# A two-layer graph network on one Trainium2 core: one-hot matrices of targets kept in 8 bits between the layers, and four more edge groups sorted

## The chip, the cores and the metric

The kernel runs on one core of one Trainium2 chip. The metric is the device time of one execution in microseconds (us). The median of three timed runs of the kernel before is 2827.05 us (2824.18 to 2834.32).

## The reference

There are 6250 nodes of 64 features and 206250 edges, sorted by their target. Two message-passing layers follow each other, each behind a layer norm and a relu and each with a residual:

```
h = relu(layernorm(x))
msg = relu(h[src] + edge_attr_16 @ W_edge.T + b_edge)
agg = segment_sum(msg, dst)
u = (h + agg) @ W1.T + b1;  u = relu(batchnorm(u)) @ W2.T + b2;  x = x + u
h = relu(layernorm(x))
msg = relu(concat(h[src], edge_attr_64) @ M_W.T + M_b)
z = segment_sum(msg, dst)
x = x + relu(concat(h, z) @ U_W.T + U_b)
```

The second layer needs, per edge, the same source and the same target as the first.

## The kernel before, in words

Edges come in NG = 101 groups of 16 tiles of 128 edges, 1612 tiles in all. The first GS = 73 groups are **sorted**: each tile's rows are scattered into a table `place` in HBM, into SB = 36 blocks by target (128 targets to a block), and in a block into 50 tiles by source. The other 28 groups are **direct**: their source rows are fetched by an indirect DMA for each tile.

*Layer 0, stage A (the loop at L929).* For each sorted group, `places` and `rank` (VectorE) compute where rows go, `rows` copies the attributes into a tile `to` of 4 buffers (ScalarE L824, L829), and `scatter` issues 16 indirect DMAs from GpSimd (L840). After each part of a group, `Blocks.step` pushes one item of a finished block, at most four in a group. An item is up to 8 tiles of 128 edges: 50 tiles make 6 items of 8 tiles and one of 2. `Line.push` runs its stages two pushes deep. `prepare` makes `hot_s`, the one-hot matrix of sources, in bf16 (L434). `gather` multiplies it into the node table split into three bf16 parts, which is 24 matmuls to a full item. `targets` makes `hot_d`, the one-hot matrix of targets, in f32 (VectorE L459). `messages` adds and applies the relu. `keep` casts `hot_s` to 8-bit floats (ScalarE L440) and stores it in `hots` in HBM. `sums`, in a later push, multiplies messages and `hot_d` into the block's sums.

*Layer 0, stage B (`unsorted`, L1046).* For each direct group GpSimd issues 16 gathers (L545), and two halves of 8 tiles go through the `Direct` class, each with a `hot_d` of its own (L595). Up to two sorted items stand ahead of each half, as long as there are any.

*Layer 1 (`unsorted` again).* A sorted item loads its 8-bit `hot_s` as `st` (6 buffers, L348 to L351), uses it as it is for the 24 matmuls, makes `hot_d` again on VectorE (L459) from the target column of the block's rows `eb` (loaded whole for each block, 2 buffers), adds its message on VectorE (L470) and applies the relu on ScalarE (L471). Four items stand ahead of each direct half, six in the first two slots, in which no direct half is due. `hot_d` and `msg` have 3 buffers here. A gather waits for a point in TensorE's work one slot back (`pace`).

TensorE, VectorE and ScalarE run in the order in which the program is written (`manual_schedule`), and so do the loads and stores that SyncE issues (`load`, L139): an instruction that waits holds all that is behind it. Blocks of `place` are filled with -1 (`fill`) before rows are scattered into them.

Of the kernel before, what the change touches and what calls it, by code (L numbers as in the profile page):

```python
# [40 lines left out]
F8 = mybir.dt.float8e4  # L41
# [5 lines left out]
P = 128  # L47
# [14 lines left out]
T = NB + 1  # L62
RW = D + ED + 2
SRC = D + ED
DST = SRC + 1
SB = 36
GS = 73
ND = NG - GS
REGION = P * T
ROWS = SB * REGION  # L70
K = 2 * NB
# [8 lines left out]
def window(g):  # L80

    return min(max((g * GT * P * N // E - 31) // P, 0), SB - 2)


LAST = [max(g for g in range(GS) if window(g) <= d <= window(g) + 1) for d in range(SB)]
FIRST = [min(g for g in range(GS) if window(g) <= d <= window(g) + 1) for d in range(SB)]


def begin(g):

    return min((g * GT + GT // 2) * P * N // E - P // 2, NP - P)


DB = begin(GS) // P
LATEST = [max(g for g in range(GS, NG) if begin(g) < (d + 1) * P) for d in range(DB, NB)]


@with_exitstack
def gnn_kernel(
# [24 lines left out]
    nc = tc.nc  # L124

    const = ctx.enter_context(tc.tile_pool(name="const", bufs=1))
    dram = ctx.enter_context(tc.tile_pool(name="dram", bufs=1, space=bass.MemoryType.DRAM))
# [4 lines left out]
    zero = until_1.enter_context(tc.tile_pool(name="zero", bufs=2))  # L132
    pools = [zero, None]
# [5 lines left out]
    def load(to, what):  # L139

        i = nc.sync.dma_start(to, what)
        return tc.keep_in_program_order(i) if in_order[0] else i
# [9 lines left out]
    def turn_slot():  # L152
        slots.append(list(products))
        products.clear()
# [8 lines left out]
    def bank(shape, name, tag, bufs=1, dtype=F32):  # L163
        return ps.tile(shape, dtype, name=name, tag=tag, bufs=bufs)
# [144 lines left out]
    def turned(attrs, n):  # L309

        p = bank([P, P], "at_p", "tr")
        at = zero.tile([P, P], F32, name="at", bufs=3)
        nc.tensor.transpose(p[:n * ED, :], attrs.rearrange("p t f -> p (t f)"), ident)
        nc.scalar.copy(at[:n * ED, :], p[:n * ED, :])  # L314
        return at
# [4 lines left out]


    src_rows = dram.tile([SB, T * P], BF16, name="src_rows")
    hots = dram.tile([P, SB, T * P], F8, name="hots")

    def columns(layer, d, eb):

        if layer == 0:
            p = bank([T, P], "st_p", "tr")
            nc.tensor.transpose(p, eb[:, :, SRC], ident)
            cols = zero.tile([T, P], BF16, name="cols")  # L330
            nc.scalar.activation(cols, p, AF.Identity, bias=shift[:, d:d + 1])
            load(src_rows[d, :].rearrange("(t p) -> t p", p=P), cols)
        dl = work.tile([P, T, 1], F32, name="dl")
        nc.vector.tensor_scalar(dl[:, :, 0], eb[:, :, DST], float(-P * d), None, op0=OP.add)
        attrs = None
        if layer == 0:
            attrs = zero.tile([P, T, ED], F32, name="attrs")
            nc.scalar.copy(attrs, eb[:, :, D:D + ED])
        return dl, attrs

    def sources(layer, d, c):


        a, b = CH[c]
        if layer == 0:
            st = zero.tile([P, 8, P], BF16, name="st", bufs=6)
        else:
            st = pools[1].tile([P, 8, P], F8, name="st", bufs=6)  # L348
        to = st[:, :b - a, :].rearrange("p t q -> p (t q)")
        if layer == 1:  # L350
            load(to, hots[:, d, a * P:b * P])  # L351
        else:
            row = src_rows[d, a * P:b * P]
            load(to, bass.AP(tensor=row.tensor, offset=row.offset, ap=[[0, P], [1, (b - a) * P]]))
        return st
# [26 lines left out]
    class Line:  # L382
# [10 lines left out]
        def push(self, item):  # L393
            now, self.now = (item, None) if self.straight else (self.now, item)
            if self.straight and item:
                item.prepare()
            if now:
                now.gather()
                now.targets()
            if self.later:  # L400
                self.later.pop(0)()
            if self.now:
                self.now.prepare()
            if now:
                now.messages()
            if self.now:
                self.now.keep()
            self.gathered.append(now)
            if len(self.gathered) > self.lag:
                last = self.gathered.pop(0)  # L410
                if last:
                    last.sums()
                    self.later = last.after[:1] + self.later + last.after[1:]
# [5 lines left out]
    class Sorted:  # L419
# [7 lines left out]

        def prepare(self):
            a, n, st = self.a, self.n, self.st
            self.hot_s = st  # L430
            if self.layer == 0:
                self.at = turned(self.attrs[:, a:self.b, :], n)
                self.hot_s = hot_s = zero.tile([P, 8, P], BF16, name="hot_s", bufs=2)
                nc.vector.tensor_scalar(hot_s[:, :n, :], st[:, :n, :], pcol, None, op0=OP.is_equal)  # L434

        def keep(self):

            n = self.n
            hot_8 = zero.tile([P, 8, P], F8, name="hot_8")
            nc.scalar.copy(hot_8[:, :n, :], self.hot_s[:, :n, :], saturate=False)  # L440
            load(hots[:, self.d, self.a * P:self.b * P],
                 hot_8[:, :n, :].rearrange("p t q -> p (t q)"))

        def gather(self):
# [11 lines left out]
        def targets(self):  # L456
            n = self.n
            self.hot_d = pools[self.layer].tile([P, 8, P], F32, name="hot_d", bufs=2 + self.layer)
            nc.vector.tensor_tensor(self.hot_d[:, :n, :],  # L459
                                    slot_p[:, None, :].to_broadcast([P, n, P]),  # L460
                                    self.dl[:, self.a:self.b, :].to_broadcast([P, n, P]),
                                    op=OP.is_equal)
# [78 lines left out]
    def gather(table, g, pool, bufs, lag):  # L541
        gat = pool.tile([P, GT, D], F32, name="gat", bufs=bufs)
        for t in range(min(GT, FULL - g * GT)):
            k = (g - GS) * GT + t
            i = nc.gpsimd.indirect_dma_start(  # L545
# [22 lines left out]
    class Direct:  # L568
# [9 lines left out]
        def prepare(self):  # L578
            pass

        def keep(self):
            pass

        def gather(self):
# [100 lines left out]
    acc = const.tile([P, NP], F32, name="acc")  # L685
# [7 lines left out]
    with tc.tile_pool(name="sort", bufs=1) as sort:  # L693
# [219 lines left out]
        for j0, j1 in chunks:  # L913
            n = j1 - j0
# [12 lines left out]
        steps = Blocks(0, line, loaded, lambda d: slot[0] - LAST[d] - 1, finish_0)  # L927
        with tc.manual_schedule(engines=ordered):
            for g in range(1, GS):  # L929
# [7 lines left out]
                d = window(g) + 3  # L937
                if d < SB and d not in fills:
                    fill(d)
                if g + 2 < GS:  # L940
# [4 lines left out]
                    to = rows(g + 2)  # L945
# [26 lines left out]
    p = bank([P, P], "most_p", "tr")  # L972
# [69 lines left out]
    p = bank([P, P], "b2_p", "tr")  # L1042
# [3 lines left out]
    def unsorted(layer, table, steps, per_half, behind, window_of, done):  # L1046

        with ExitStack() as stack:  # L1050
            pool = stack.enter_context(tc.tile_pool(name=f"unsorted{layer}", bufs=1))
            pools[1] = pool
            stack.enter_context(tc.manual_schedule(engines=ordered))
            line = steps.line
            gats, eas = {}, {}
            left = list(range(DB, NB))
            for g in range(GS, NG + behind):
                turn_slot()
                if g == GS and layer == 1:
                    slots.clear()  # L1060
                if g < NG:
                    gats[g] = gather(table, g, pool, 4 + layer, 1)
                if g > GS and g <= NG:
                    eas[g - 1] = attributes(layer, g - 1, pool)
                c = g - behind
                pd = Bank("pd", ("rk", "pa")[g % 2]) if layer else Bank("pd", "rk")
                for h in range(2):
                    for _ in range(per_half + 2 * layer * (c < GS)):
                        steps.step()
                    if c < GS:  # L1070
                        continue
                    now = []
                    if h == 1:
                        now = [d for d in left if LATEST[d - DB] <= c
                               and (d >= SB or steps.i == len(steps.list))]
                        left = [d for d in left if d not in now]
                    after = [f for d in now for f in done(d)]
                    line.push(Direct(layer, c, h, gats[c], eas[c], pd, window_of(c), pool, after))
            while steps.step():
                pass  # L1080
            line.later += [f for d in left for f in done(d)]
            line.flush()
# [49 lines left out]
    table1 = dram.tile([NP, D], F32, name="table1")  # L1132
# [147 lines left out]
    line_1 = Line(2, True)  # L1280
    line_1.later += [f for n in nodes for f in n.plain()]
    steps = Blocks(1, line_1, lambda d: load_block(d)[0], lambda d: 3, finish_1)
    unsorted(1, table1[:, :], steps, 4, 2, lambda g: acc[:, begin(g):begin(g) + P], update)

    def more_1(k, b, delta, pool):
        node = ds(b * P + k * NH * P, P)
# [75 lines left out]
```

## Time and profile before

The profiled execution took 2824.5 us, with a span of 2822.7 us.

| stretch of the span | what runs | us |
|---|---|---|
| 31.8 to 1602.6 | 1168 scatters on GpSimd (stage A) | 1570.8 |
| 1608.8 to 2163.2 | 444 gathers of layer 0 (stage B) | 554.4 |
| 2163.2 to 2225 | batch norm, layer norm, node table of layer 1 | 62 |
| 2225 to 2787.1 | 444 gathers of layer 1 | 562 |
| 2787.1 to 2822.7 | last items, outputs, end | 35.6 |

| 100 us from | PE | DVE | ACT | POOL | granted clock | DMA share |
|---|---|---|---|---|---|---|
| 900 (of 300, a third) | 71.0 | 62.8 | 35.0 | 76.9 | 0.86 | 0.79 |
| 1900 | 59.4 | 21.2 | 12.4 | 75.5 | 0.77 | 0.32 |
| 2400 | 94.4 | 99.6 | 35.8 | 75.8 | 1.00 | 0.78 |

A busy time is the time in which the engine executes. GpSimd's 75 to 77 of 100 is all that it reaches, because 0.30 us of issue stand between two of its indirect DMAs. The DMA share is the mean busy share of the core's 16 DMA engines.

### The profile page before, as it was taken

Reading aid. Unit: us, or ns where it says so; the run is one execution under the profiler, and the core shown is the slowest. Engines: PE = TensorE matmul, PEld = TensorE weight load, DVE = VectorE, ACT = ScalarE, POOL = GpSimd, SP = SyncE. Lnnn points to the kernel's source line nnn. Section 1 sums busy time; section 2 is a strip of 40 time slices with the busy share of each in tenths; the row PEclk is TensorE's granted clock in tenths of the full one; section 3 lists DMA queues with packets and bytes.
Section 4 is the critical chain, followed back from the end, with each engine's and each line's share of the span. In section 5 each row is a group of like instructions: output and inputs, shape, how many; then the busy total and the mean of one; then the engine's idle time right before and its main releaser. Section 6 shows DMA issues by size and latency. Waiting matters only on the chain. (4 is left out here: it accounts for less than half of the span.)

```text
span 2822.7 us, 57117 instructions
## 1 busy us (share of the span) xinstructions
PE 1974.5 (70%) x20820; PEld 1540.6 (55%) x20820; DVE 1693.4 (60%) x3624; ACT 848.2 (30%) x1637; POOL 2051.0 (73%) x2066
## 2 busy tenths in 40 slices
PE   2366667567766766756677498656565699999887
PEld 2354555455554655545556366444343577878776
DVE  7755656565755756665666244222222599999887
ACT  2232333233333333323334233111111223333332
POOL 5777777777777777777777677777775377777773
PEclk8687888788988988878889799677777899999999
DMA  9877886878888878677776664333332487787764
GB/s 221 199 217 192 233 223 177 207 210 228 210 215 220 225 216 225 192 201 213 222 220 200 179 199 125 90 82 88 87 84 72 144 272 261 247 269 254 249 229 130
DMA packets 343316, 545.17 MB, mean 193 GB/s; under 512 B 114416, under 2 KB 248944, under 8 KB 333808
## 3 DMA queue, kind: packets, MB, share of 16 engines
q1 hardware_dynamic: 270256, 461.35, 55.8%
q0 software_dynamic: 65792, 78.27, 11.4%
q10 hardware_dynamic: 6976, 1.80, 0.4%
q8 instruction: 166, 2.72, 0.4%
q14 instruction: 126, 1.03, 0.1%
HBM read 362.45 MB, written 178.74 MB: 192 GB/s over the span
## 5 line engine op out<-in xcount | busy, mean ns | idle before, releaser
L840 POOL DMA_INDIRECT place<-to,ix x1168 | 1197.4, 1025 | 398.1 <-issue 262.0
L545 POOL DMA_INDIRECT gat<-table,src_d x888 | 845.6, 952 | 331.6 <-issue 181.6
L459 DVE TENSOR_TENSOR hot_d<-cbank,dl 128x1024 f32<-128x1024 f32 (+1 forms) x504 | 556.2, 1104 | 540.6 <-PE pa L148 415.6
L148 PE MATMUL pa<-hot_d,msg 128*64 128x128 f32 (+1 forms) x5400 | 719.3, 323 | 16.6 <-ACT msg L471 15.3
L148 PEld LDWEIGHTS pa<-hot_d,msg 128*64 128x64 f32 (+1 forms) x5400 | 556.4, 163 | 80.6 <-ACT msg L471 25.3
L148 PE MATMUL gp<-we,at 128*128 128x512 f32 (+1 forms) x504 | 293.1, 667 | 401.3 <-ACT at L314 401.3
L148 PEld LDWEIGHTS gp<-we,at 128*128 128x128 f32 (+1 forms) x504 | 90.5, 215 | 420.0 <-ACT at L314 412.9
L148 PEld LDWEIGHTS <-hot_s 128*128 128x128 bf16 x5400 | 222.5, 106 | 160.8 <-issue 143.1
L440 ACT CAST hot<-hot_s 128x1024 fp8e4<-128x1024 bf16 (+1 forms) x252 | 240.6, 955 | 128.7 <-DMA hots<-hot 73.3
L471 ACT ACTIVATE msg<-msg 128x512 f32<-128x512 f32 (+1 forms) x252 | 147.0, 584 | 305.0 <-DVE msg L470 292.3
L608 DVE TENSOR_TENSOR msg<-pm_d,gat 128x512 f32<-128x512 f32 (+1 forms) x56 | 38.4, 686 | 327.8 <-DMA gat<-table,src_d 326.8
L148 PE MATMUL gp<-tab,hot_s 128*128 128x64 bf16 x5400 | 231.8, 205 | 0.0
L148 PE MATMUL gp<-tab,st 128*128 128x64 bf16 x5400 | 205.1, 195 | 32.7 <-DVE msg L470 12.4
L148 PEld LDWEIGHTS <-st 128*128 128x128 fp8e4 x5400 | 176.3, 99 | 77.4 <-issue 63.8
L148 PE MATMUL pm_d<-we,ea_d 128*128 128x512 f32 x112 | 93.1, 926 | 167.2 <-DVE msg L608 167.2
L824 ACT COPY to<-raw 128x288 f32<-128x288 f32 x73 | 31.7, 434 | 589.5 <-DMA place<-to,ix 541.4
L148 PEld LDWEIGHTS pm<-we,ea 128*128 128x128 f32 x1168 | 164.6, 207 | 18.4 <-ACT to L824 11.7
L148 PE MATMUL pm<-we,ea 128*128 128x128 f32 x1168 | 166.5, 291 | 11.6 <-DMA ea<-in_ea 11.6
L470 DVE TENSOR_TENSOR msg<-gp,eb 128x512 f32<-128x512 f32 (+1 forms) x252 | 158.0, 627 | 4.1 <-PE gp L148 3.9
L595 DVE TENSOR_TENSOR hot_d<-cbank,rel_d 128x1024 f32<-128x1024 f32 x112 | 135.4, 1209 | 20.5 <-PE pa L148 13.0
L468 ACT ACTIVATE msg<-gp 128x512 f32<-128x512 f32 (+1 forms) x252 | 140.1, 556 | 11.3 <-PE gp L148 9.9
L609 ACT ACTIVATE msg<-msg 128x512 f32<-128x512 f32 (+1 forms) x56 | 35.1, 626 | 348.0 <-DVE msg L608 347.4
(181 smaller groups left out, 2247.4 us busy)
## 6 DMA issues: line engine op xcount, KB each, us to landing
eb<-place SPq DMA_DIRECT2D x72, 2050.0 KB
place<-minus SPq DMA_DIRECT2D x180, 410.0 KB
st<-src_rows SPq DMA_DIRECT2D x216, 256.0 KB
ea<-in_ea SPq DMA_DIRECT2D x73, 512.0 KB
hots<-hot SPq DMA_DIRECT2D x216, 128.0 KB
st<-hots SPq DMA_DIRECT2D x216, 128.0 KB
place<-to,ix POOLq DMA_INDIRECT x1168
ea_d<-in_ea SPq DMA_DIRECT2D x28, 512.0 KB
```

Of the source, the lines that this page charges most:

```text
L148: i = nc.tensor.matmul(*args, **kwargs)
L440: nc.scalar.copy(hot_8[:, :n, :], self.hot_s[:, :n, :], saturate=False)
L459: nc.vector.tensor_tensor(self.hot_d[:, :n, :], slot_p[:, None, :].to_broadcast([P, n, P]), self.dl[:, self.a:self.b, :].to_broadcast([P, ...
L468: nc.scalar.activation(msg[:, :n, :], gp[:, :n, :], AF.Relu)
L470: nc.vector.tensor_add(msg[:, :n, :], gp[:, :n, :], self.eb[:, self.a:self.b, 0:D])
L471: nc.scalar.activation(msg[:, :n, :], msg[:, :n, :], AF.Relu)
L545: i = nc.gpsimd.indirect_dma_start(out=gat[:, t, :], out_offset=None, in_=table, in_offset=bass.IndirectOffsetOnAxis(ap=src_d[:, k:k + 1], ...
L595: nc.vector.tensor_tensor(self.hot[:, :n, :], slot_p[:, None, :].to_broadcast([P, n, P]), rel_d[:, self.k:self.k + n, None].to_broadcast([ ...
L608: nc.vector.tensor_add(msg, self.pm[:, :n, :], self.gat[:, half, :])
L609: nc.scalar.activation(msg, msg, AF.Relu)
L824: nc.scalar.copy(to[:, :, D:RW], raw)
L840: i = nc.gpsimd.indirect_dma_start(out=place[:, :], out_offset=bass.IndirectOffsetOnAxis(ap=ix[:, t:t + 1], axis=0), in_=to[:, t, :], in_o ...
```

## The change

Layer 0 stores both one-hot matrices: `hots` has two planes for each block, and `keep(1)`, called at the end of each push, casts `hot_d` to 8 bits and stores it in the second plane. The tile `hot_8` of the casts has 3 buffers where it had 2. Layer 1 loads both planes with `st`, 256 KB to a full item where it was 128 KB, and `targets` there is a ScalarE copy from 8 bits to f32 instead of VectorE's comparison; the target column `dl` is no longer made in layer 1. GS goes from 73 to 77 and SB from 36 to 38, so four groups move from direct to sorted. In layer 1, five items stand ahead of each direct half instead of four.

```diff
-SB = 36
-GS = 73
+SB = 38
+GS = 77
...
-    hots = dram.tile([P, SB, T * P], F8, name="hots")
+    hots = dram.tile([P, SB, 2, T * P], F8, name="hots")
...
+        if layer == 1:
+            return None, None
         dl = work.tile([P, T, 1], F32, name="dl")
...
-            st = pools[1].tile([P, 8, P], F8, name="st", bufs=6)
-        to = st[:, :b - a, :].rearrange("p t q -> p (t q)")
-        if layer == 1:
-            load(to, hots[:, d, a * P:b * P])
-        else:
+            st = pools[1].tile([P, 2, 8, P], F8, name="st", bufs=6)
+            load(st[:, :, :b - a, :].rearrange("p k t q -> p k (t q)"), hots[:, d, :, a * P:b * P])
...
             if self.now:
                 self.now.keep()
+            if now:
+                now.keep(1)
...
-        def keep(self):
+        def keep(self, k=0):
+            if self.layer == 1:
+                return
             n = self.n
-            hot_8 = zero.tile([P, 8, P], F8, name="hot_8")
-            nc.scalar.copy(hot_8[:, :n, :], self.hot_s[:, :n, :], saturate=False)
-            load(hots[:, self.d, self.a * P:self.b * P],
+            hot_8 = zero.tile([P, 8, P], F8, name="hot_8", bufs=3)
+            nc.scalar.copy(hot_8[:, :n, :], (self.hot_s if k == 0 else self.hot_d)[:, :n, :],
+                           saturate=False)
+            load(hots[:, self.d, k, self.a * P:self.b * P],
                  hot_8[:, :n, :].rearrange("p t q -> p (t q)"))
...
             self.hot_d = pools[self.layer].tile([P, 8, P], F32, name="hot_d", bufs=2 + self.layer)
+            if self.layer == 1:
+                nc.scalar.copy(self.hot_d[:, :n, :], self.st[:, 1, :n, :])
+                return
             nc.vector.tensor_tensor(self.hot_d[:, :n, :],
...
-    unsorted(1, table1[:, :], steps, 4, 2, lambda g: acc[:, begin(g):begin(g) + P], update)
+    unsorted(1, table1[:, :], steps, 5, 2, lambda g: acc[:, begin(g):begin(g) + P], update)
```

More of the change, by code (lines that the diff above doesn't have):

```diff
@@ L347, in sources @@
         else:
-            st = pools[1].tile([P, 8, P], F8, name="st", bufs=6)
-        to = st[:, :b - a, :].rearrange("p t q -> p (t q)")
-        if layer == 1:
-            load(to, hots[:, d, a * P:b * P])
-        else:
+            st = pools[1].tile([P, 2, 8, P], F8, name="st", bufs=6)
+            load(st[:, :, :b - a, :].rearrange("p k t q -> p k (t q)"), hots[:, d, :, a * P:b * P])
+        if layer == 0:
+            to = st[:, :b - a, :].rearrange("p t q -> p (t q)")
             row = src_rows[d, a * P:b * P]
@@ L429, in prepare @@
             a, n, st = self.a, self.n, self.st
-            self.hot_s = st
-            if self.layer == 0:
+            if self.layer == 1:
+                self.hot_s = st[:, 0]
+            else:
                 self.at = turned(self.attrs[:, a:self.b, :], n)
@@ L458, in targets @@
             self.hot_d = pools[self.layer].tile([P, 8, P], F32, name="hot_d", bufs=2 + self.layer)
+            if self.layer == 1:
+                nc.scalar.copy(self.hot_d[:, :n, :], self.st[:, 1, :n, :])
+                return
             nc.vector.tensor_tensor(self.hot_d[:, :n, :],
@@ L579, in prepare, with keep @@
             pass
-        def keep(self):
+        def keep(self, k=0):
             pass
```

## The prediction

> **What bounds the kernel now.** I read first the page's busy times and costliest groups, then the busy time by stretch, then the waits of stage A, then the order of time on TensorE in layer 1.
>
> ```profile
> PE 1974.5 (70%) x20820; PEld 1540.6 (55%) x20820; DVE 1693.4 (60%) x3624; ACT 848.2 (30%) x1637; POOL 2051.0 (73%) x2066
> ...
> L840 POOL DMA_INDIRECT place<-to,ix x1168 | 1197.4, 1025 | 398.1 <-issue 262.0
> L545 POOL DMA_INDIRECT gat<-table,src_d x888 | 845.6, 952 | 331.6 <-issue 181.6
> L459 DVE TENSOR_TENSOR hot_d<-cbank,dl 128x1024 f32<-128x1024 f32 (+1 forms) x504 | 556.2, 1104 | 540.6 <-PE pa L148 415.6
> ...
> L440 ACT CAST hot<-hot_s 128x1024 fp8e4<-128x1024 bf16 (+1 forms) x252 | 240.6, 955 | 128.7 <-DMA hots<-hot 73.3
> L471 ACT ACTIVATE msg<-msg 128x512 f32<-128x512 f32 (+1 forms) x252 | 147.0, 584 | 305.0 <-DVE msg L470 292.3
> ```
>
> GpSimd's two groups hold it nearly from end to end: 0.30 us of issue stand between two indirect DMAs. 1168 scatters in 1570.8 us are 1.345 us each, 444 gathers in 554.4 us 1.249, and in layer 1 444 in 562 us 1.266.
>
> ```profile
> 2230.00:2250.00 20.00, 13.84 (x228) 12.91 (x228) 13.38 (x25) 3.59 (x7) 15.13 (x17) 0.93 0.82 240
> 2250.00:2270.00 20.00, 18.32 (x329) 16.37 (x328) 16.21 (x28) 4.27 (x9) 15.12 (x17) 0.98 0.97 296
> 2270.00:2290.00 20.00, 15.40 (x261) 13.49 (x257) 15.41 (x28) 4.25 (x8) 15.12 (x17) 0.87 0.90 263
> ...
> 2400.00:2500.00 100.00, 94.40 (x1893) 80.57 (x1891) 99.57 (x152) 35.80 (x65) 75.83 (x80) 1.00 0.78 255
> ...
> 600.00:1500.00 900.00, 626.04 (x5420) 481.26 (x5416) 553.47 (x1382) 310.90 (x615) 688.53 (x672) 0.84 0.80 217
> ```
>
> The columns are PE, PEld, DVE, ACT and POOL, then granted clock, DMA share and GB/s. In stage A (last row) only GpSimd is full. In layer 1 VectorE (99.57 of 100) and GpSimd are both full, and TensorE is near it.
>
> ```profile
> ACT to L824 <- DMA place<-to,ix: 329.1, 38, 22.2
> ...
> 2403.22 0.76 PEld L148 LDWEIGHTS <-st 128*128 128x128 fp8e4 x24 [0.17 <-issue]
> 2403.22 0.87 PE L148 MATMUL gp<-tab,st 128*128 128x64 bf16 x24
> ...
> 2404.02 0.85 PEld L148 LDWEIGHTS pa<-hot_d,msg 128*64 128x64 f32 x16
> 2404.03 1.09 PE L148 MATMUL pa<-hot_d,msg 128*64 128x128 f32 x16
> ...
> 2405.05 0.76 PEld L148 LDWEIGHTS <-st 128*128 128x128 fp8e4 x24 [0.17 <-issue]
> ```
>
> The first line (600 to 1500 us) says that ScalarE waits for a scatter to free a buffer of `to`: 329.1 us over the 42 groups there, 7.8 us a group, which is its spare time. The other lines give TensorE's price of a full layer-1 item without a gap: 2403.22 to 2405.05 is 1.83 us, of which 1.02 are the sums.
>
> **The change part by part.** *Groups moved, layer 0.* Tiles sorted go from 1168 to 1232, tiles gathered from 444 to 380. Stage A gains 64 x 1.345 = 86 us, stage B loses 64 x 1.249 = 80: +6 us. What moves with them (two blocks of fills, loads and items, `places` and `rank` four times) runs at stage A's rates inside those 86 us.
>
> *Second store, layer 0.* A full item gets one more cast. Its f32 source is not in the trace; the bf16 one took 1.048 us (395 ns for two tiles), an f32 copy of 128x800 took 0.846, VectorE's pass over 128x1024 f32 took 1.217. I take 1.05, with 0.85 and 1.22 as ends. The 123 full and 20 short items between 600 and 1500 us cost 137 us, 3.3 us a group, from the 7.8 spare. The cast also waits for `hot_8`, now three buffers for two casts a push where it was two for one; such waits were 45 us (33.2 + 11.4) in 42 groups, and if they treble that is 2 us a group more. Behind a waiting cast on ScalarE stand the next copies into `to`, and GpSimd waits for those; SyncE holds the stores behind a cast and the next `st` behind those. Spare time of 2.5 us a group remains, so I cost it at nothing. DMA: 128 pieces of 1 KB at 51 ns over 16 engines are 0.41 us an item, 1.4 us a group of 21.5, so the share goes from 0.80 to some 0.87. Cover gone, each us a group too many costs 77 us.
>
> *VectorE, layer 1.* All 278 us of L459 go, and the 7.5 us of `dl`. What stays for 266 items (228 full) is 228 x 0.684 + 38 x 0.284 = 167, the 47.5 direct halves at 1.218 + 0.691 = 91, and 45 of sums and outputs: 303 us against 552 before. VectorE stops being a bound.
>
> *ScalarE, layer 1.* 8 bits to f32 is again not in the trace; same ends, 1.05 taken. 228 x (1.05 + 0.63) + 38 x (0.39 + 0.31) + 47.5 x 0.63 + 38 x 0.25 = 449 us. A full item costs 1.68 us, under TensorE's 1.83; at 1.22 it would be 1.85, level with it. The copy stands in order behind the previous item's relu, but the sums that need it come two pushes later.
>
> *GpSimd, layer 1.* 380 x 1.266 = 481 us against 562: 81 us less.
>
> *TensorE, layer 1.* 228 x 1.83 + 38 x 0.46 + 47.5 halves x 1.03 + 49 outputs x 0.43 + 11 for the plain products = 516 us; the same sum for before gives 502. So with GpSimd and VectorE relieved, TensorE gains work, and its floor stands above GpSimd's.
>
> *DMA, layer 1.* The trace's packets between 2230 and 2790 us, by size: 16400 bytes (`eb`) 676 ns, 1 KB (`st`) 52, 256 bytes (short `st`) 18, gathers 128 (2 KB each), 4 KB (terms) 206; all else 47 us. Over 16 engines: `eb` 38 x 128 x 676 = 205 us; `st` 228 x 256 x 52 = 190; short ones 11; gathers 6080 x 128 = 49; terms 24 x 128 x 206 = 40; the rest 47. The sum is **541 us**; the same sum for before gives 440, of which the window shows 430. This is now the longest, 25 us over TensorE.
>
> *The sum.* Loads of layer 1 start at 2225 + 6 = 2231. How full can the engines be? The three stretches where loads held TensorE up (2230 to 2290) show 0.82, 0.97, 0.90. I take 0.97, the best, since in the steady part there are six `st` and two `eb` in flight and no node stores; the mean, 0.90, is the low end. 541 / 0.97 = 558, so the last load lands at 2789. Three items, the output and the end follow; from TensorE's last matmul (2812.7) to the end are now 10 us, so I put 15. Span 2804, and with the 1.8 us around it (2824.5 - 2822.7) **2806 us**, 19 below the profiled 2824.5. The median of the runs shown is 2.5 above the profiled time; I leave the number as it is.
>
> Two rules, beside this sum. The trace grants TensorE 1.00 of its clock at 2410 to 2430 us and 0.91 at 2390 to 2410, where its busy time fell from 18.59 to 17.45. The Trainium skill (TensorE: Matmul & The Clock Gate, Part 1) says that the clock falls to half after a window of about 3.4 us without work; by that rule loads that come late are paid twice, and a stall of 1.8 us in one block of two would add an estimated 34 us. The skill also holds (Perfetto Trace Analysis, Identifying the Most-Contended Engine) that weight-load busy time measures TensorE's headroom better than matmul busy time: 80.57 against 94.40 here, so its floor would be nearer 0.81 of the window and the TensorE rival below lower by as much; the rows without a gap speak for 1.83 us an item.
>
> **The rivals.** *TensorE holds layer 1, loads hide.* This needs loads that overlap better than their packet times say. For it: slices of the page that move 269 GB/s in layer 1 are not yet full. Against it: 541 over 516. First item at 2227.3 + 6, 516 us at 0.97 to 1.00 (it was full at 20.00 of 20 from 2290 to 2310) and 10 to the end: 2761 to 2777 with 1.8 around it; I say **2772**.
>
> *Loads get dearer as the queue fills, and it is slower.* `eb` takes 799 ns in stage A at a share of 0.80, and 752 at 2235 to 2290. At 0.90 of the engines, layer 1's loads take 601 us: 2231 + 601 + 15 + 2 = **2849**. With `eb` at 752 alone the work is 564, at 0.95 2842. It decides when loads need over 576 us, the point of no gain. Against it: from 2300 on, `eb` holds 666 ns at 0.78.
>
> *Layer 0 gives the gain back.* If casts and their waits take 0.5 us a group over the spare time, stage A grows by 38 us: **2844**. Against it are the 7.8 us; for it, that ScalarE, SyncE and TensorE wait for each other in a fixed order, so one late store is felt by all.
>
> *It doesn't do what it says:* GpSimd still holds layer 1. Then its end is 2231 + 481, with two slots of work behind it (20 items, 4 halves, 41 us) and 10: 2763, which is no slower than TensorE's case; it cannot be what keeps the time up.
>
> **How the numbers follow.** The forecast, 2806 (own range 2785 to 2822), 0.45; TensorE's case 0.26; dear loads 0.21; layer 0 0.08. 0.5% is 14 us, about what a measurement of this kernel can tell from no change: under 2811 is faster, over 2839 slower. The forecast puts 0.30 of its 0.45 under 2811, and TensorE's case is all there: 0.56. Dear loads put 0.17 over 2839, layer 0 0.06: slower 0.23. The rest, 0.21, is the same. The range, 2764 to 2848, runs from TensorE's case without idle time nearly to the loads at 0.90.
>
> **What would show it.** Right: a DMA share of 0.93 or more from 2300 us on, `st<-hots` as what TensorE and ScalarE wait for, VectorE near 55 of 100, gathers that wait for TensorE instead of issue, scatters at 1.34 us each. Wrong: `eb` over 720 ns or a granted clock under 0.95 in layer 1 (slower), a share under 0.9 with TensorE over 97 of 100 (faster), or scatters that wait for ScalarE's `to` in stage A.

## The result, and the profile after

The changed kernel takes 2916.86 us (2909.75 to 2922.26) beside 2828.69 us: 1.0314 times the kernel before, interval 1.0297 to 1.0331. The forecast was 2806, with a range to 2848. The profiled execution spans 2911.8 us, 89.1 more than before.

The page of the changed kernel, engines and groups (the same columns as before):

```profile
PE 2026.5 (70%) x21572; PEld 1583.4 (54%) x21572; DVE 1489.2 (51%) x3430; ACT 1318.2 (45%) x2219; POOL 1977.4 (68%) x2002
...
L850 POOL DMA_INDIRECT place<-to,ix x1232 | 1248.0, 1013 | 497.7 <-issue 257.0
L555 POOL DMA_INDIRECT gat<-table,src_d x760 | 721.7, 950 | 350.0 <-issue 152.1
...
L446 ACT CAST hot<-hot_d 128x1024 fp8e4<-128x1024 f32 (+1 forms) x266 | 254.3, 956 | 687.2 <-DMA hots<-hot 686.4
```

GpSimd executes less than before (1977 against 2051 us) in a longer span, so it no longer sets the pace alone. The last line is the new thing: the 266 new casts execute for 254 us, and ScalarE sits idle for 687 us ahead of them, 686 of it until a store of `hots` has landed. With the waits ahead of the first cast these are 696 us; before, they were 73 us in all.

| step | before | forecast | after |
|---|---|---|---|
| scatters, one after the other | 1.345 us | 1.345 | 1.394 (1717.1 us for 1232) |
| gathers of layer 0 | 1.249 | 1.249 | 1.286 (488.6 us for 380) |
| layer 1's first gather starts | 2225.6 | 2232 | 2312.2 |
| from there to the end of the span | 597.1 | 573 | 599.6 |

So two things went wrong: what runs ahead of layer 1 came out 80 us longer than forecast, and layer 1, forecast 24 us shorter than before, is 2.5 us longer.

Waits between 600 and 1500 us of the changed kernel (us in total, times, longest):

```profile
ACT hot L446 <- DMA hots<-hot: 409.8, 99, 14.4
PEld gp L148 <- ACT at L314: 229.6, 58, 12.4
DVE hot_d L469 <- ACT hot L446: 223.5, 38, 14.4
```

The line that led here before, ScalarE's copy into `to` waiting for a scatter (329.1 us in this window), is down to 31.5 us in the whole span. The spare time has become a wait for stores, and TensorE and VectorE wait behind it. ScalarE, then SyncE, in order of time at one such place:

```profile
1000.84 1.05 ACT L446 CAST hot<-hot_s 128x1024 fp8e4<-128x1024 bf16 x1
1014.28 1.04 ACT L446 CAST hot<-hot_d 128x1024 fp8e4<-128x1024 f32 x1 [12.39 <-DMA hots<-hot]
1015.23 0.58 ACT L839 COPY to<-pm 128x512 f32<-128x512 f32 x1
```

```profile
1000.80 1.23 SPq L141 DMA_DIRECT2D hots<-hot  x2
1002.08 0.87 SPq L141 DMA_DIRECT2D place<-minus  x1
1003.57 0.73 SPq L141 DMA_DIRECT2D eb<-place  x1
1005.17 0.32 SPq L141 DMA_DIRECT2D st<-src_rows  x1
1008.89 17.59 SPq L141 DMA_DIRECT2D hots<-hot  x6
```

A cast stands for 12.39 us until a buffer is free. The store that frees it is the first of the two at 1000.80; it lands 13.4 us after its issue. In between SyncE issues the 2 MB load of a block (`eb`, at 1003.57), so the load was not ahead of this store but beside it. The six stores behind the load take 17.59 us to go out, and five of them wait for their casts in turn. Behind the cast stands the copy into `to` that a scatter needs.

In layer 1, two stretches of 100 and 112 us (PE, PEld, DVE, ACT, POOL, granted clock, DMA share, GB/s):

```profile
2400.00:2500.00 100.00, 93.83 (x1910) 81.90 (x1909) 51.63 (x90) 74.33 (x114) 72.84 (x77) 0.98 0.96 322
...
2800.00:2912.00 112.00, 91.53 (x1852) 79.32 (x1848) 53.10 (x100) 72.03 (x110) 17.91 (x19) 0.95 0.70 233
```

VectorE is relieved as forecast (99.6 to 51.6 of 100), and TensorE is not faster for it: 93.8 against 94.4. The DMA engines are at 0.96.

### The profile page after: what moved, and what is told of

It is laid out like the page before. It is cut to its first block, busy times and chain, and to the rows that moved or that the text cites. A ratio compares the mean times of both kernels' runs of the same rounds, so it can differ in the third digit from the quotient of the medians.

```text
span 2911.8 us, 60021 instructions
## 1 busy us (share of the span) xinstructions
PE 2026.5 (70%) x21572; PEld 1583.4 (54%) x21572; DVE 1489.2 (51%) x3430; ACT 1318.2 (45%) x2219; POOL 1977.4 (68%) x2002
## 5 line engine op out<-in xcount | busy, mean ns | idle before, releaser
L850 POOL DMA_INDIRECT place<-to,ix x1232 | 1248.0, 1013 | 497.7 <-issue 257.0
L555 POOL DMA_INDIRECT gat<-table,src_d x760 | 721.7, 950 | 350.0 <-issue 152.1
L148 PE MATMUL pa<-hot_d,msg 128*64 128x128 f32 (+1 forms) x5700 | 790.3, 330 | 3.0 <-DVE acc L381 2.4
L148 PEld LDWEIGHTS pa<-hot_d,msg 128*64 128x64 f32 (+1 forms) x5700 | 604.9, 166 | 69.2 <-ACT hot L446 2.6
L469 DVE TENSOR_TENSOR hot_d<-cbank,dl 128x1024 f32<-128x1024 f32 (+1 forms) x266 | 294.7, 1108 | 640.2 <-ACT hot L446 369.8
L446 ACT CAST hot<-hot_d 128x1024 fp8e4<-128x1024 f32 (+1 forms) x266 | 254.3, 956 | 687.2 <-DMA hots<-hot 686.4
L467 ACT CAST hot_d<-st 128x1024 f32<-128x1024 fp8e4 (+1 forms) x266 | 250.0, 940 | 34.1 <-DMA st<-hots 15.9
L481 ACT ACTIVATE msg<-msg 128x512 f32<-128x512 f32 (+1 forms) x266 | 155.0, 583 | 73.7 <-DVE msg L480 70.6
L313 PE MATMUL at_p<-ident,attrs 128*128 128x128 f32 (+1 forms) x266 | 87.7, 330 | 143.2 <-ACT acc L881 142.6
L148 PE MATMUL pm_d<-we,ea_d 128*128 128x512 f32 x96 | 75.3, 877 | 120.0 <-DVE msg L618 120.0
```

The source lines that it names most:

```text
L148: i = nc.tensor.matmul(*args, **kwargs)
L446: nc.scalar.copy(hot_8[:, :n, :], (self.hot_s if k == 0 else self.hot_d)[:, :n, :], saturate=False)
L467: nc.scalar.copy(self.hot_d[:, :n, :], self.st[:, 1, :n, :])
L469: nc.vector.tensor_tensor(self.hot_d[:, :n, :], slot_p[:, None, :].to_broadcast([P, n, P]), self.dl[:, self.a:self.b, :].to_broadcast([P, ...
L481: nc.scalar.activation(msg[:, :n, :], msg[:, :n, :], AF.Relu)
L555: i = nc.gpsimd.indirect_dma_start(out=gat[:, t, :], out_offset=None, in_=table, in_offset=bass.IndirectOffsetOnAxis(ap=src_d[:, k:k + 1], ...
```

## The experiments

**Four runs on a slow chip (e1 to e4).** The kernel before took 3549.86 us there as well, against 2801 to 2834 elsewhere, so their times, one each, can't be read beside the others and decide nothing here. Their expectations, and the times:

e1, six buffers, 3560.31 us: 

> The changed kernel with six buffers for the 8-bit casts instead of three (and one buffer instead of two for the layer norm's h at the start, to make room). Theory A (the casts on ScalarE wait for a buffer whose store still stands behind megabytes of loads, and hold the copies for the scatters): the 686 us of waits on stores fall under 200, the 1232 scatters take 1650 to 1670 us instead of 1717, time about 2835 to 2850. Rival B (the added store traffic itself slows all DMAs) and rival C (the casts' own time on ScalarE is too much): within 15 us of 2913.

e2, cast without store, 3515.65 us: 

> The second cast is made, its store is left out; layer 1 loads the first plane twice, so it uses the sources' matrices in place of the targets' (the same work on wrong data). Theory A: no cast waits long, scatters 1650 to 1670 us, time about 2835. Rival B: the same. Rival C (ScalarE's time): no change, 2913.

e3, store without cast, 3530.33 us: 

> The second cast is left out and the first cast's tile is stored into both planes, so layer 1 again uses the sources' matrices for the targets'; the DMA traffic is that of the changed kernel, with three buffers for one cast a push. Theory A: waits under 250 us, scatters near 1660 us, time about 2840. Rival B (traffic): no change, 2913. Rival C: about 2840.

e4, one plane loaded, 3521.56 us: 

> Layer 0 as changed; layer 1 loads only the first plane (128 KB to a full item) and ScalarE turns that one to f32 in place of the targets' matrix, so 95 us of the 541 us of DMA work in layer 1 go and all engines keep their work. If the DMA engines bound layer 1 (theory A): its 600 us fall to 550 to 565, time about 2870. Rival (TensorE's own order and waits for ScalarE's copies bound it): 590 to 600, time 2905 to 2913.

In the table of the others, "start" is where layer 1's first gather begins in the profile, so it measures layer 0, and "layer 1" is the rest of the span. The kernel before took medians of 2804 to 2807 us on these chips; its profile was taken on none of them. A ratio without an interval is of single times. Starts are best compared on one chip.

| run | chip | ratio to before | start | layer 1 |
|---|---|---|---|---|
| e5 six buffers (one time) | 3 | 1.0033 | 2214.0 | 600.8 |
| e6 one plane (one time) | 3 | 1.0057 | 2236.2 | 585.3 |
| e7 changed kernel | 1 | 1.0083 (1.0057 to 1.0109) | 2236.8 | 593.3 |
| e8 six buffers | 1 | 1.0032 (1.0018 to 1.0046) | 2208.9 | 597.9 |
| e9 cast, no store | 1 | 1.0023 (1.0010 to 1.0036) | 2208.6 | 601.5 |
| e10 store, no cast | 1 | 1.0015 (0.9998 to 1.0031) | 2211.8 | 596.3 |
| e11 two parts on TensorE | 14 | 1.0064 (1.0041 to 1.0087) | 2240.0 | 579.9 |
| e12 73 groups | 14 | 1.0087 (1.0058 to 1.0117) | 2222.3 | 604.4 |
| e13 before, 77 groups | 14 | 0.9993 (0.9965 to 1.0020) | 2206.8 | 581.5 |
| e14 every second item | 14 | 0.9969 (0.9952 to 0.9987) | 2208.8 | 593.7 |
| e15 two buffers | 9 | 1.0320 (1.0298 to 1.0342) | 2292.1 | 596.7 |
| e16 four buffers | 9 | 1.0061 (1.0041 to 1.0081) | 2216.6 | 601.5 |
| e17 a third of the items | 9 | 0.9948 (0.9931 to 0.9964) | 2212.6 | 579.9 |
| e18 as e13, longer | 9 | 0.9981 (0.9969 to 0.9993) | 2214.0 | 587.5 |

**Layer 0: how deep the ring of casts is (e5, e7, e8, e15, e16).** The theory was that the ring of buffers costs the time; the rivals were the store traffic itself and the casts' own time.

```diff
-            hot_8 = zero.tile([P, 8, P], F8, name="hot_8", bufs=3)
+            hot_8 = zero.tile([P, 8, P], F8, name="hot_8", bufs=6)    # 2 in e15, 4 in e16
...
-            h = ln.tile([P, 8, D], F32, name="h", bufs=2)
+            h = ln.tile([P, 8, D], F32, name="h", bufs=1)             # with six alone
```

> Once more six buffers for the 8-bit casts instead of three (one buffer instead of two for the layer norm's h at the start), since the chip of the first look took 3549.86 us for the kernel before as well. Theory A (casts on ScalarE wait for a buffer whose store stands behind loads, and hold the copies for the scatters): waits on stores fall from 686 us under 200, the scatters take 1650 to 1670 us instead of 1717, time 2835 to 2850. Rivals B (the store traffic slows all DMAs) and C (the casts' own time on ScalarE): within 15 us of 2913.

> The changed kernel once more, beside the others of this call on one chip, because stage A's scatters took 1717 us in its profile but 1645 us in the one-plane run, whose stage A is the same. If theory A (the ring of three) is right, ScalarE waits over 500 us on stores here too, and the ratio to before lies over that of six buffers by 1% or more. If the 72 us were the chip's, the ratio comes to 1.005 to 1.015 and six buffers give the same within 0.5%.

> Six buffers for the 8-bit casts (one for h), on the same chip. Theory A: ratio to before 1.00 to 1.01, waits on stores under 50 us, ScalarE's spare time back as a wait for scatters. Rivals B and C: as the changed kernel.

> The changed kernel with two buffers for the 8-bit casts instead of three. Theory (the loss of layer 0 is the wait for a buffer, and it is small on this chip only because ScalarE's spare time of 7 to 8 us a group still covers most of it): with two buffers the cover is gone, as it was in the first profile; layer 1's gathers start at 2290 or later instead of 2237, ratio 1.025 or more. Rival (the 75 us between the first profile and the later ones have nothing to do with the ring): within 10 us of the changed kernel, 1.008.

> The changed kernel with four buffers for the casts, so two for each cast of a push as before the change. Theory: waits on stores fall under 150 us, layer 1's gathers start at 2210 to 2218, ratio 1.003 to 1.005. Rival (depth matters little beyond three): 2230 or later.

The waits on stores, first in the changed kernel (e7), then with six buffers (e8), two (e15) and four (e16), each with ScalarE's wait for a scatter beside it:

```profile
ACT hot L446 <- DMA hots<-hot: 610.1, 174, 15.2
ACT to L834 <- DMA place<-to,ix: 74.1, 9, 19.7
```

```profile
ACT to L834 <- DMA place<-to,ix: 563.8, 64, 21.7
...
ACT hot L446 <- DMA hots<-hot: 5.5, 3, 3.0
```

```profile
ACT hot L446 <- DMA hots<-hot: 688.5, 197, 16.6
ACT to L834 <- DMA place<-to,ix: 48.3, 7, 16.3
```

```profile
ACT to L834 <- DMA place<-to,ix: 541.3, 70, 21.7
ACT hot L446 <- DMA hots<-hot: 96.9, 50, 17.1
```

With four or six buffers ScalarE waits for scatters, as before the change: GpSimd sets the pace. With two or three it waits for stores, and the two waits together grow from 569 us (six) to 638, 684 and 737. Layer 1 starts at 2292, 2237, 2217 and 2209 us with 2, 3, 4 and 6 buffers. On one chip each, three buffers start it 28 us later than six (e7, e8) and 22 us (e6, e5; e6 changes layer 1 alone), and 33 us later than no second store (e11, e13; e11 too changes layer 1 alone). Against e18, which has no second store, four buffers cost 3 us and two 78 (e16, e15). So hundreds of microseconds of waits cost little as long as they only take the place of spare time.

The two buffers of e15 came out as the theory said (2290 or later, 1.025 or more), and so did the six of e8, with waits on stores under 50 us and a ratio under 1.01. e5's time, 2816.61 us, lies under the 2835 to 2850 expected, which were reckoned from the times of the first chip. e16 met its start and its waits (96.9 us); its ratio, 1.0061, lies over the 1.003 to 1.005 expected, which its interval takes in.

e7 was a miss: the theory asked for a ratio 1% or more over that of six buffers, and it lies 0.5% over it. Its 1.0083 is inside the 1.005 to 1.015 that I had given for a loss that is the chip's. So on this chip three buffers cost 28 us, where the first profile came out 80 us over the forecast. Something of the chips does differ: a 1640-byte piece of a fill takes 115 ns between 600 and 1500 us of the first profile and 105 in e7, a 4 KB piece 230 and 213, a 16400-byte piece 782 and 772. That longer DMAs are why the ring ran dry further in the first profile fits e15, which loses 78 us by one buffer fewer, but no run on the first chip has a deeper ring. That the ring made the whole 80 us there stays argued; that ScalarE waited 686 us for stores there is in its trace.

**Layer 0: cast or store (e9, e10).**

```diff
+            if k == 1:
+                return                       # e9: ahead of the second store; e10: of the second cast
...
-            load(..., hots[:, d, :, a * P:b * P])
+            load(..., hots[:, d, 0:1, a * P:b * P].to_broadcast([P, 2, (b - a) * P]))   # e9
...
+            load(hots[:, self.d, 1, ...], hot_8[...])                 # e10: the one cast stored twice
```

> Three buffers, second cast made, its store left out, layer 1 loads the first plane twice (sources in place of targets). Theory A: layer 0 as with six buffers, within 10 us. Rival B (store traffic): 20 us or more under six buffers. Rival C (ScalarE's time): as the changed kernel.

> Three buffers, the second cast left out, the first cast's tile stored into both planes (layer 1 uses sources in place of targets): the changed kernel's DMA traffic. Theory A: layer 0 within 15 us of six buffers. Rival B: as the changed kernel. Rival C: under six buffers by 20 us or more.

Both start layer 1 about as early as six buffers do (2208.6 and 2211.8 against 2208.9), as the theory said. e13, without either, starts at 2206.8 on another chip. So neither the 250 us of casts nor the 31 MB of stores costs more than some 5 us on these chips; both rivals fall there. Only the two together in a ring of three do.

**Layer 1: what bounds it now (e6, e11).**

```diff
-            load(st[:, :, ...], hots[:, d, :, a * P:b * P])
+            load(st[:, 0, ...], hots[:, d, 0, a * P:b * P])          # e6
...
-                nc.scalar.copy(self.hot_d[:, :n, :], self.st[:, 1, :n, :])
+                nc.scalar.copy(self.hot_d[:, :n, :], self.st[:, 0, :n, :])   # e6
...
-                for k in range(3):
+                for k in range(3 - layer):                           # e11
```

> Once more layer 0 as changed, while layer 1 loads only the first plane and turns that one to f32 (sources in place of targets): 95 us of 541 us of DMA work in layer 1 go, all engines keep their work. If the DMA engines bound layer 1: its 600 us fall to 550 to 565, time about 2870. Rival (TensorE's order and its waits for ScalarE bound it): 590 to 600, time 2905 to 2913.

> The changed kernel, but layer 1 multiplies the sources' matrices into two parts of the node table instead of three (8 of 24 matmuls of a full item left out, so the third part's digits are missing; loads, casts and VectorE as changed): 228 x 0.27 = 61 us of TensorE's work go. Theory (TensorE with its short waits bounds layer 1): from the first gather of layer 1 to the end 593 us fall to 545 to 565. Rival (DMA engines at 0.94 bound it): 580 or more. If both matter alike: 565 to 580.

The steady stretch of layer 1 in the changed kernel (e7), with one plane (e6) and with two parts (e11):

```profile
2306.00:2793.00 487.00, 453.79 (x9211) 395.56 (x9212) 250.37 (x439) 361.63 (x552) 312.51 (x328) 0.98 0.94 317
```

```profile
2306.00:2784.00 478.00, 449.32 (x9157) 391.82 (x9154) 249.74 (x436) 358.61 (x546) 312.08 (x327) 0.99 0.79 265
```

```profile
2310.00:2779.00 469.00, 410.04 (x7445) 348.81 (x7444) 246.58 (x433) 354.93 (x545) 314.27 (x328) 0.96 0.96 324
```

The changed layer 1 itself takes 593 to 602 us in its six profiles (the first one, e5, e7, e8, e15, e16), so differences of some 8 us say little. Taking 95 us of loads away frees 8 us against e7 and 15.5 against e5 on its own chip (one time): the DMA share falls from 0.94 to 0.79, and TensorE goes from 453.8 of 487 (0.93) to 449.3 of 478 (0.94). Leaving out a third of the small matmuls, 61 us by my sum, takes 42 us off TensorE's busy time in layer 1 (526.9 to 484.5) and frees 13 to 22 us: TensorE falls to 0.87, and the DMA share rises to 0.96. For e6, 585 us lies nearer to the rival than to my theory; for e11, 579.9 lies on the edge between "both alike" and the rival, and far from the theory. So neither resource alone bounds layer 1. That each is held up by the other in turn fits the shares, but no run relieves both, so what is left over when one goes is argued.

**The change taken apart (e12, e13, e18).**

```diff
-SB = 38
-GS = 77
+SB = 36
+GS = 73                                                              # e12, with 4 items to a half
```

> The changed kernel with 73 groups and 36 blocks sorted and four items ahead of a half, as before. Theory (the groups moved are neutral in layer 0 and only exchange one bound for another in layer 1): layer 1 takes 585 to 600 us, bound by GpSimd's 444 gathers (562 us) and the tail; layer 0 loses the same 25 us by the ring; ratio 1.005 to 1.010. Rival (the four groups gain what the forecast said): layer 1 20 us or more slower than the changed kernel's 593.

> The kernel before with 77 groups and 38 blocks sorted and five items ahead of a half, targets' matrices still made on VectorE in layer 1. Theory: VectorE's work in layer 1 grows from 535 us by 14 items and falls by 8 halves, so layer 1 stays at 595 to 610; layer 0 without the second store gains no loss beyond the 6 us; ratio 1.00 to 1.01. If the copy on ScalarE was worth something at 77 groups, this is slower in layer 1 than the changed kernel's 593.

> The kernel before with 77 groups and 38 blocks sorted and five items ahead of a half, targets on VectorE, timed longer: its first runs lay in two clusters (2790 to 2795 and 2806 to 2807 us). Expected 0.995 to 1.000; the changed kernel's copy on ScalarE is then worth a loss of 0.5% or more against it.

e13 and e18 are the kernel before with the two constants raised and five items to a half.

e12: the 8-bit targets without the groups moved give 1.0087, and a layer 1 of 604 us. I had said 585 to 600, the rival 613 or more; its gathers alone take 569 us (2222.3 to 2791.3). e13 and e18: the groups moved without the 8-bit targets give 0.9993 (0.9965 to 1.0020) and, in more runs, 0.9981 (0.9969 to 0.9993), and a layer 1 of 581 to 588 us, less than the 595 to 610 I expected of e13 and less than the changed kernel's 593 to 602. e18's ratio lies in the 0.995 to 1.000 expected. VectorE is full in e13, and TensorE a little fuller (0.95) than in e6 and e7, where ScalarE makes all copies:

```profile
2276.00:2748.00 472.00, 447.27 (x9066) 384.86 (x9064) 464.01 (x696) 167.88 (x310) 312.65 (x326) 1.00 0.79 263
```

So a VectorE at 98% costs layer 1 no more time than DMA engines at 94%, and moving the groups is the part of the change that gains, by some 0.2%.

**A share of the copies (e14, e17).** With six buffers, only some items keep their targets in 8 bits; the others make them on VectorE.

```diff
+            if c % 3 == 0:                                           # e17; c % 2 in e14
                 load(st[:, :, ...], hots[:, d, :, a * P:b * P])
+            else:
+                load(st[:, 0, ...], hots[:, d, 0, a * P:b * P])
...
-            if self.layer == 1:
+            if self.layer == 1 or k == 1 and not ((self.a // 8) % 3 == 0):
                 return
...
-            if self.layer == 1:
+            if self.layer == 1 and (self.a // 8) % 3 == 0:
                 nc.scalar.copy(self.hot_d[:, :n, :], self.st[:, 1, :n, :])
```

> Every second item keeps its targets' matrix in 8 bits and turns it on ScalarE, the others make it on VectorE as before; six buffers for the casts, 77 groups. Half of the added DMA work (48 us in layer 1), half of ScalarE's copies, VectorE at some 440 of 590 us. If loads and ScalarE's copies held TensorE up in layer 1: 570 to 580 us there, ratio 0.99. If TensorE's own work and the start of the stage bound it: 585 to 595, ratio 1.000 to 1.003.

> 77 groups, six buffers, and items 0, 3 and 6 of a block (two full ones and the short one of 7) keep their targets' matrix in 8 bits; the others make it on VectorE. VectorE at some 83% of layer 1, DMA share near 0.83, TensorE at 0.94. If an even load of the engines is what counts in layer 1: 575 to 585 us there, ratio 0.993 to 0.998. If every load taken off VectorE costs as much on DMA: as the kernel before with 77 groups, 0.998 to 1.000.

e14 is at 0.9969, which neither of its two cases gave; its profile's layer 1 (593.7) missed the 570 to 580 and lies in the rival's 585 to 595, but that execution took 2804.25 us, and others of it 2790. e17 came out as expected for an even load, and is a little faster than both kernels: 0.9948 (0.9931 to 0.9964), 2791.58 us. On its chip e18 took 2800.16. Its steady stretch:

```profile
2282.00:2752.00 470.00, 445.94 (x9038) 389.88 (x9036) 387.54 (x595) 235.78 (x407) 313.43 (x327) 0.98 0.86 285
```

VectorE is at 0.82, the DMA share at 0.86, TensorE at 0.95.

## Why the prediction was wrong

- *Second store, layer 0: this step failed.* "If they treble that is 2 us a group more ... I cost it at nothing." The waits went from 73 to 696 us in the whole span (45 to 410 between 600 and 1500 us), over nine times, not three. I scaled the waits of a ring with one cast a push instead of asking how long a store takes to land. Two casts a push with three buffers leave a store one and a half pushes. A push took 6.3 us on average before (143 items in 900 us), but casts come in bursts: the four from 996.51 to 1000.84 started within 4.3 us. Of the 176 stores that a cast waited for, half took 7.0 us or more from issue to landing, the longest 17.4. In 31 of these waits (262 us), the longest of 14.4 us among them, a block load of 2 MB was issued between the store and its landing; in 36 (193 us) at most 15 us ahead of the store; in the other 109 (242 us) neither. The spare 7.8 us a group went into the waits, then time of GpSimd's scatters, and of stage B, whose gathers slowed to 1.286 us each. Price: 80 us against the forecast in the first profile, 22 to 33 us on three other chips.
- The cast itself was right: 1048 ns against 1.05 us for f32 to 8 bits, 1031 for 8 bits to f32. The 6 us for the groups moved are not shown: there is no profile of the kernel before on the chips of the experiments. With three buffers and on one chip, layer 1 starts at 2222.3 with 73 groups and at 2240.0 with 77 (e12, e11), 18 us apart, which holds the ring's cost for four more groups too.
- *How full the engines can be: this step failed too.* 541 us of DMA work was right (0.91 of the 591 us from 2312 to 2903 is 538; `eb` took 681 ns and 1 KB pieces 52). But I divided by 0.97, the best of three rows of 20 us, for the whole stage, with only 15 us behind the last load. The steady stretch gives 0.94, the first 70 us 0.91 to 0.92 with TensorE at 51 of 70, and the last 20 to 30 us hold hardly a load (0.19 from 2880 to 2900). From the first gather to the end were 599.6 us where I had 573. The path was wrong too, and not only the share: without 95 us of this work (e6) layer 1 is only 8 to 16 us shorter, so its loads do not set its length alone. A share of 0.93 or more, which I had named as a sign of being right, came (0.94) without the gain.
- *TensorE, layer 1:* 516 us by the sum, 530 by the profile, a difference of the size of what the clock lost (0.96 instead of 1.00). Its case in the rivals (2772) supposed that it could run at 0.97 to 1.00; e6, with loads at 0.79, has it at 0.94. In one stretch of 20 us (2740 to 2760) its busy time was 16.5 us and its granted clock 0.83. Between 2382 and 2873 the trace has its clock at half five times, for 3.4 or 6.8 us, each time behind 1.9 to 3.7 us without a matmul or a weight load. The Trainium skill (TensorE: Matmul & The Clock Gate, Part 1), by which a window of about 3.4 us without work halves the clock, agrees in direction; in this trace pauses from 1.9 us on did it. My estimate of 34 us by that page took stalls of 1.8 us, which are shorter than its window, so it did not follow from it.
- *Dear loads* as a rival is refuted in its cause: pieces of 16400 bytes held 681 ns at a share of 0.91. Its share of 0.90 for the whole stage came nearer than my 0.97.
- *Layer 0 gives the gain back* named the right place and direction, with a chance of 0.08 and 38 us. It is what happened in the first profile, at twice the price.
- VectorE (303 us forecast, 290 measured) and ScalarE (449 forecast, 406 as busy time) were near, and neither was full: 0.51 and 0.74 of the steady stretch in e7.

## What to carry to other kernels

When a stage gets a second producer for a ring of buffers, count the ring in time: how soon a buffer is needed again where uses follow each other most closely, against the longest time a store takes to land while the largest loads are under way, and not by the waits seen so far. Relieving one full engine is worth only the distance to the next resource. With VectorE at 0.98 and TensorE at 0.95 (e13), moving a third of the work (e17) brought 0.3% against e18 on one chip, and moving all of it (e8) ended at 1.0032 of the kernel before, where e18 has 0.9981. Of a change with two parts, price each alone: here the groups moved gained some 0.2%, and the copy that was to make room for them cost it back.

## What the runs showed of the hardware

- The cost of a ring of three differs between chips for the same program: 80 us against the forecast in the first profile, 28 us against six buffers in e7, where the pieces of DMAs between 600 and 1500 us differ by 1 to 10%. With two buffers another chip (e15) loses 78 us. Spare time hides a cost up to an edge; that the edge lies in another place on another chip fits these times and is not shown.
- One chip ran all kernels some 26% slower, the kernel before too (3549.86 us). In e1 GpSimd was busy as long as elsewhere (1972.3 us against 1980.5 in e5), as VectorE and ScalarE were, TensorE longer (2254 against 2007 us, at a granted clock of 0.78 against 0.85). So most of the 744 us by which its span is longer than that of e5 is waits; their cause stays open.
